# Two-layer graph attention in float32: the last step's combination of layer 0 set earlier, and its transposes placed directly behind a set of q and k

## The chip, the cores and the metric

The kernel runs on one core of a Trainium2 chip. The time is device time in microseconds (us) for one launch, given as the median of several runs. A profiled execution of the same program shows what each engine did: TensorE (PE for matmuls, PEld for its weight loads), VectorE (DVE), ScalarE (ACT), GpSimd (POOL) and SyncE (SP), which issues most of the transfers.

## The reference

There are 64 graphs of 256 nodes with 512 features, and an adjacency matrix for each. Two attention layers follow each other, both with a layer norm and a ReLU in front and a residual sum behind.

```python
# layer 0: 4 heads of 64
h = jnp.maximum(_layernorm(x), 0.0)
q, k, v = split_heads(h @ Wq), split_heads(h @ Wk), split_heads(h @ Wv)
sim = jnp.where(adj[:, None], jnp.einsum('bhid,bhjd->bhij', q, k) * 64 ** -0.5, -finfo.max)
x = x + (softmax(sim) @ v, heads joined) @ Wo + bo

# layer 1: 8 heads of 64, a second layer norm with gamma and beta inside, the diagonal always allowed
h = jnp.maximum(_layernorm(x), 0.0)
h = _layernorm(h) * gamma + beta
q, k, v = split(h @ w_qkv.T)
scores = jnp.where((adj | eye)[:, None], jnp.einsum('bihd,bjhd->bhij', q, k) * 64 ** -0.5, -1e9)
x = x + (softmax(scores) @ v, heads joined) @ w_out.T + b_out
```

(The excerpt is shortened; all of it is float32.)

## The kernel before

The 64 graphs are taken two at a time, in 32 steps (s = 0 to 31). A step has 512 tokens, which are four row blocks of 128. Two heads of 64 make a pair; layer 0 has pairs 0 and 1, layer 1 has pairs 0 to 3. The work of a step consists of the following pieces.

- `load_x` (L485) fetches the residual rows `xt`, and `first_bias` (L490) adds the bias of layer 0 to them on POOL, in four additions (L493).
- `project_qk` (L743) makes q and k of two pairs at once. It splits the product into 2x2 blocks and uses seven block products where the plain way needs eight. I call the seven products a **set**. Each product is four matmuls in float32, which the profile records as eight (L755). The products come in the order 1, 6, 5, 2, 7, 3, 4 (`SET`). Each is evicted from PSUM before it can be used: products 1 and 2 by ACT (L689, L697), products 6, 5, 7, 3 and 4 by DVE (L691, L693, L695, L699, L701). `bank_of` (L729) lets product 2 add into product 1's PSUM bank, product 3 into product 5's, and product 4 into product 7's, so product 4 can begin only when product 7 has been evicted, by L695.
- `project_v1` (L788) and `combine1` (L813) are sets too: v of layer 1 (L796), and the output projection of layer 1 (L821). `combine0` (L803) is the output projection of layer 0, in the plain way: two matmuls for each row block (L807), and the sum with `xt` on DVE (L811).
- `visit` (L986) handles one pair's attention between two sets. It weighs the values of the pair whose probabilities are ready (`weigh_out`, matmuls L896, copy on ACT L914), sums its keys (`key_sums`, L930, from the half sums `pd` that `key_halves` makes at L887), inverts the sums on DVE (`invert`, L940 and L941), sends the inverses to all rows by eight transfers on SP (L955, into the tile `invb`, which has one buffer), and multiplies them in on POOL (`normalise`, L960). For the next pair it makes the scores (L853), masks them on DVE (`mask_scores`, L877) and exponentiates on ACT (`exponentials`, L882).
- `norm1` (L615) and `norm1_rest` (L630) are the two nested layer norms before layer 1. For each row block: statistics of `xt` on DVE (L569, L570), the negated mean on ACT (L623), centring and ReLU into `h` on ACT (L624), statistics of `h` on DVE. Then for two row blocks at a time five small operations on POOL (L639, L640, and L579 to L581 in `row_scales`), and `scale_row` (L583) on ACT (L585).
- `transpose_h` (L644) turns `h` by 16 transposes on PE (L651), four for each block of 128 features; ACT (L661) and DVE (L657) evict them into `hT`. `act_sums0` and `act_sums1` (L407 to L413) make the four sums of blocks that a set needs.

The order of instructions on PE, DVE, ACT and POOL is written out by hand. Every piece is put into a list by `at(period, place, ...)`, `at_set` spreads the seven products of a set over one unit of place, and at the end the list is sorted by `period * 6.13 + place`. In one period of 6.13 units, step s does layer 1 while step s+1 finishes layer 0 and step s+2 begins it, so that a set of one step covers the DVE, ACT and POOL work of another. Each engine then runs its own list in order; semaphores make it wait for what it needs. SP has its transfers in order as well. The last period (p = 30) is special: step 30 finishes, step 31 must do the whole of its layer 1, and there is no step 32 whose work could cover it.

In that period the order on PE is: q and k of step 30's pairs 0 and 2 (place 0), v of step 30 (1), q and k of its pairs 1 and 3 (2), then `combine0` of step 31 (3), a visit (3.685), the transposes of step 31 (3.8), q and k of step 31's pairs 0 and 2 (`LAST_QK` = 4), `combine1` of step 30 (5), q and k of step 31's pairs 1 and 3 (6), v of step 31 (7), all four weighings (8) and `combine1` of step 31 (8.1). A visit stands ahead of each set up to place 3, and others between the products of later sets.

```python
            at_dense(p, AT_C0 + 0.01 + 0.14 * t - back, 0.14, combine0, s, t)
            at(p, AT_C0 + 0.3 + 0.14 * t - back if (s, t) != (NSTEP - 1, 3) else 3.69, norm1, s, t)
```

Of the kernel before, what the change touches and what calls it, by code (L numbers as in the profile page):

```python
# [315 lines left out]
def fast_path(  # L316
# [19 lines left out]
    nc = tc.nc  # L336
# [70 lines left out]
    def act_sums0(b, eng=nc.gpsimd):  # L407
        eng.tensor_tensor(b[:, 3], b[:, 7], b[:, 0], ALU.subtract)
# [334 lines left out]
    def project_qk(s, lyr, a, n):  # L743

        st = S[s]
        half, w = (PR0, PR1)[lyr] // 2, (wqk0, wqkv1)[lyr]
        if n == 1:
            for pr in (a, a + half):
                st["qk", lyr, pr] = sm.tile([P, 2, T], FP, name="qk", bufs=3)
        t0, t1 = st["qk", lyr, a], st["qk", lyr, a + half]  # L750
        bank, first = bank_of(st, ("qk", a), n, N)
        wa, ba = PRODUCT[n]
        for k in range(2):
            for c in range(HC):
                nc.tensor.matmul(  # L755
                    bank[:, k, :], w[:, wa, c, k, a * P:(a + 1) * P], st["hT"][:, ba, c, :],
                    start=first and (k, c) == (0, 0), stop=(k, c) == (1, HC - 1),
                    skip_group_check=True,
                )

        def rest():
            evacuate(n, bank, (t0[:, :, :N], t0[:, :, N:], t1[:, :, :N], t1[:, :, N:]))
            if lyr == 0 and n in (3, 4):
                t = t0 if n == 3 else t1
                nc.gpsimd.tensor_tensor(t[:, 0, :], t[:, 0, :], st["ne"], ALU.mult)
        return rest
# [203 lines left out]
    def at(period, place, fn, *args):  # L970
        events.append((period * PERIOD + place, len(events), fn, args))

    def at_dense(period, place, length, fn, *args):

        rest = []
        at(period, place, lambda: rest.append(fn(*args)))
        at(period, place + length - LAST, lambda: rest[0]())

    def at_set(period, place, order, fn, *args):
        for i, n in enumerate(order):  # L980
            at_dense(period, place + i / 7, 1 / 7, fn, *args, n)
# [1 line left out]
    SET = (1, 6, 5, 2, 7, 3, 4)  # L983
    SETC = (1, 5, 2, 6, 7, 3, 4)

    def visit(period, w, prev, cur, later=0.0):  # L986

        w -= 0.0003
        if 0 <= prev[0] < NSTEP:
            at(period, w, weigh_out, *prev)  # L990
            at(period, w, key_sums, *prev[:3])
            at(period, w + later, invert, *prev[:3])
            at(period, w + (0.63 if prev[1:3] == (1, 1) else 0.55), normalise, *prev[:3])
        if 0 <= cur[0] < NSTEP:
            at(period, w, scores, *cur)
            at(period, w + later, mask_scores, *cur, 0)
            at(period, w + 0.05, exponentials, *cur, 0)
            at(period, w + 1 / 7, mask_scores, *cur, 1)
            at(period, w + 0.18, exponentials, *cur, 1)
            at(period, w + 0.2, key_halves, *cur, 0)  # L1000
            at(period, w + 0.3, key_halves, *cur, 1)

    AT_C0, AT_Q0, AT_V0, AT_H1, AT_C1 = 3.0, 3.57, 4.57, 5.13, 5.131
    LAST_QK = 4.0
    for s in range(-1, NSTEP - 1):
        p, tail = s, s == NSTEP - 2
        if s >= 0:
            visit(p, 0.0, (s + 1, 0, 0, True), (s + 1, 0, 1))
            visit(p, 1.0, (s + 1, 0, 1, False), (s, 1, 0))
        visit(p, 2.0, (s, 1, 0, True), (s, 1, 2))  # L1010
        visit(p, 3.0, (s, 1, 2, False), (s, 1, 1))
        visit(p, 3.685 if tail else AT_Q0 + 2 / 7, (s, 1, 1, False), (s, 1, 3), 0.03 if tail else 0.0)
        if s >= 0:
            visit(p, LAST_QK + 3 / 7 if tail else AT_V0, (s, 1, 3, False), (s + 2, 0, 0))

    none = (NSTEP,)
    p = NSTEP - 2
    for w, i, pr in (
        (LAST_QK + 1, 5 / 7, 0), (LAST_QK + 1 + 3 / 7, 5 / 7, 2), (LAST_QK + 3, 5 / 7, 1), (LAST_QK + 3 + 2 / 7, 4 / 7, 3)
    ):  # L1020
        visit(p, w, none, (NSTEP - 1, 1, pr))
        at(p, w + i - 0.0005, key_sums, NSTEP - 1, 1, pr)
        at(p, w + i, invert, NSTEP - 1, 1, pr)
    for i, pr in enumerate((0, 1, 2, 3)):
        at(p, LAST_QK + 4 + 0.01 * i, weigh_last, pr)

# [5 lines left out]
    for s in range(NSTEP):  # L1032
# [33 lines left out]
        p = s - 1  # L1066
        if s == 0:
            p -= 2.23 / PERIOD
        at(p, 1.0 if s else 0.0, load_x, s)
        at(p, 1.8 if s else 1.55, first_bias, s)  # L1070
        back = 0.0 if s else 0.13
        for t in range(NT):
            at_dense(p, AT_C0 + 0.01 + 0.14 * t - back, 0.14, combine0, s, t)
            at(p, AT_C0 + 0.3 + 0.14 * t - back if (s, t) != (NSTEP - 1, 3) else 3.69, norm1, s, t)
            at(p, ((3.55, 3.7, 4.05, 4.2) if s < NSTEP - 1 else (3.55, 3.6, 3.7, 3.705))[t] - back, norm1_rest, s, t)
            at(p, 3.62 + 0.08 * t if 0 < s < NSTEP - 1 else 6.5 + 0.1 * t, second_bias, s, t)
            at(p, 4.5 + 0.1 * t if 0 < s < NSTEP - 1 else (4.25 if s == 0 else 3.71) + 0.003 * t, scale_row, s, t)

        for c in range(NC):
            at(p, (AT_H1 if s < NSTEP - 1 else 3.8) + 0.0001 * c, transpose_h, s, 1, c)  # L1080
        at(p, AT_C1 + 0.15 if s < NSTEP - 1 else 3.95, lambda s=s: act_sums0(S[s]["hT"], nc.gpsimd if s < NSTEP - 1 else nc.vector))
        at(p, AT_C1 + 0.5 if s < NSTEP - 1 else 3.96, lambda s=s: act_sums1(S[s]["hT"], nc.gpsimd if s < NSTEP - 1 else nc.vector))
        p = s
        if s < NSTEP - 1:
            at_set(p, 0.0, SET, project_qk, s, 1, 0)
            at_set(p, 1.0, SET, project_v1, s)
            at_set(p, 2.0, SET, project_qk, s, 1, 1)
            last = s == NSTEP - 2
            at(p, 4.55 if not last else LAST_QK + 0.99, lambda s=s: act_sums0(S[s]["oT1"]))
            at(p, AT_C1 + 0.1 if not last else LAST_QK + 1.0, lambda s=s: act_sums1(S[s]["oT1"]))  # L1090
            at_set(p, AT_C1 if not last else LAST_QK + 1, SETC, combine1, s)
            at(p, 6.3, store, s)
        else:
            p = s - 1
            at_set(p, LAST_QK, SET, project_qk, s, 1, 0)
            at_set(p, LAST_QK + 2, SET, project_qk, s, 1, 1)
            at_set(p, LAST_QK + 3, SET, project_v1, s)
            at(p, LAST_QK + 4.015, lambda s=s: act_sums0(S[s]["oT1"], nc.vector))
            at(p, LAST_QK + 4.035, lambda s=s: act_sums1(S[s]["oT1"], nc.vector))
            at_set(p, LAST_QK + 4.1, (1, 5, 2, 3, 6, 7, 4), combine1, s)  # L1100
            for n, (i, j) in enumerate(((0, 0), (0, 1), (1, 1), (1, 0))):
                at(p, LAST_QK + 4.1 + (3, 6, 6, 7)[n] / 7, store_block, s, i, j)
# [69 lines left out]
```

## Time and profile before

| | |
|---|---|
| median of 3 runs | 3401.17 us (3400.61 to 3402.93) |
| the profiled execution: its time, its span | 3401.54 us, 3399.3 us |
| PE busy | 3373.3 us, 99% of the span |
| PEld, DVE, ACT, POOL busy | 77%, 56%, 37%, 59% |
| transfers | 173.89 MB, 51 GB/s in the mean |
| the chain of work that ended last | PE 97%, DVE 1% |

The page gives busy time by engine over the whole span. The chain of work that ended last is followed back from the last instruction, at each step to what released it. The timeline lists instructions of one engine in order of time: start, length, line and operation, and in brackets the idle time before it with what ended that. Matmuls overlap, and their ends are modelled. The windows table gives busy time and the granted PE clock (1.00 is full speed) in stretches of time.

### The profile page before, as it was taken

How to read it: one execution, taken by the hardware profiler on the slowest of the kernel's cores; microseconds unless marked ns; L12 is line 12 of the kernel's file. 1: busy time of each engine (PE TensorE's matmuls, PEld its weight loads, DVE VectorE, ACT ScalarE, POOL GpSimd, SP SyncE). 2: the span in 40 equal slices, each digit the busy share in tenths (PEclk: the TensorE clock that was granted, in tenths of full speed). 3: DMA queues.
4: the chain of work that ended last, by engine and by line, in shares of the span. 5: the costliest groups of instructions: out<-in, count | busy, mean ns of one | idle time of the engine just before them, and what ended most of it. 6: DMA issues, size and time to landing. Idle time of an engine off the chain costs nothing.

```text
span 3399.3 us, 59198 instructions
## 1 busy us (share of the span) xinstructions
PE 3373.3 (99%) x22602; PEld 2621.7 (77%) x22602; DVE 1919.5 (56%) x3402; ACT 1243.2 (37%) x2193; POOL 1991.2 (59%) x1858
## 2 busy tenths in 40 slices
PE   8999999999999999999999999999999999999999
PEld 6777777787777877778777777777787777877777
DVE  6755556555565555555555655556555555555565
ACT  4433443333333334433344333343333443334431
POOL 5655665556655556655576556665555655556632
PEclk9999999999999999999999999999999999999999
DMA  4111111211111211111111111111121111111111
GB/s 129 46 56 57 48 39 46 58 57 54 32 48 56 58 54 33 48 55 56 58 43 44 46 58 57 53 32 48 57 58 52 34 47 57 57 58 41 32 41 42
DMA packets 167697, 173.89 MB, mean 51 GB/s; under 512 B 59624, under 2 KB 112368, under 8 KB 167408
## 3 DMA queue, kind: packets, MB, share of 16 engines
q1 hardware_dynamic: 167008, 169.78, 16.9%
q8 instruction: 180, 2.95, 0.4%
q14 instruction: 109, 0.89, 0.1%
q10 hardware_dynamic: 400, 0.27, 0.0%
HBM read 85.99 MB, written 33.62 MB: 35 GB/s over the span
## 4 chain that ended last, share of the span: by engine, by line
PE 97%; DVE 1%; ACT 0%; issue 0%; DMA 0%; POOL 0%; SPq 0%; DVEq 0%; POOLq 0%
PE mm L755 34%; PE mm L796 12%; PE mm L821 11%; PE sc L853 11%; PE sc L896 10%; PE mm L782 6%; PE mm L807 6%; PE mm L651 3%; PE mm L930 2%; PE mm L543 0%; DVE bs L569 0%; ACT h L585 0%; DVE wqk L405 0%; DVE wqkv L405 0%; DVE inv L940 0%
## 5 line engine op out<-in xcount | busy, mean ns | idle before, releaser
L887 POOL TENSOR_TENSOR pd<-p 128x512 f32<-128x512 f32 x378 | 477.2, 1278 | 631.6 <-ACT p L882 523.3
L755 PE MATMUL mm<-hT,wqkv 128*128 128x256 f32 x3584 | 800.0, 382 | 2.6 <-DVE hT L411 1.4
L755 PEld LDWEIGHTS mm<-hT,wqkv 128*128 128x128 f32 x3584 | 673.8, 190 | 112.6 <-issue 23.1
L882 ACT ACTIVATE p<-p 128x512 f32<-128x512 f32 x768 | 459.1, 629 | 478.8 <-DVE p L877 477.9
L940 DVE RECIPROCAL inv<-mm 128x128 f32<-128x128 f32 x384 | 339.7, 926 | 367.6 <-PE mm L930 330.9
L877 DVE TENSOR_TENSOR p<-sc,n 128x512 f32<-128x512 f32 x768 | 481.2, 682 | 4.2 <-PE sc L853 4.2
L914 ACT COPY oT<-sc 128x512 f32<-128x512 f32 x188 | 110.2, 586 | 993.6 <-PE sc L896 993.6
L755 PE MATMUL mm<-hT,wqk 128*128 128x256 f32 x1792 | 403.4, 382 | 0.7 <-ACT wqkv L468 0.6
L796 PE MATMUL mm<-wqkv,hT 128*128 128x256 f32 x1792 | 396.1, 381 | 0.0
L821 PE MATMUL mm<-wo,oT 128*128 128x256 f32 x1792 | 393.3, 379 | 1.0 <-DVE xt L712 0.7
L960 POOL TENSOR_TENSOR oT<-oT,invb 128x512 f32<-128x512 f32 x188 | 240.9, 1282 | 261.0 <-DMA invb<-inv 253.3
L755 PEld LDWEIGHTS mm<-hT,wqk 128*128 128x128 f32 x1792 | 338.4, 191 | 69.5 <-DVE inv L940 9.9
L853 PE MATMUL sc<-qk 64*128 64x256 f32 x3072 | 384.1, 389 | 0.0
L796 PEld LDWEIGHTS mm<-wqkv,hT 128*128 128x128 f32 x1792 | 337.6, 190 | 56.3 <-issue 11.4
L821 PEld LDWEIGHTS mm<-wo,oT 128*128 128x128 f32 x1792 | 337.6, 190 | 47.7 <-issue 1.5
L896 PE MATMUL sc<-p,v 128*32 128x256 f32 x6144 | 370.7, 382 | 0.0
L853 PEld LDWEIGHTS sc<-qk 64*128 64x128 f32 x3072 | 281.2, 186 | 104.2 <-issue 77.6
L896 PEld LDWEIGHTS sc<-p,v 128*32 128x32 f32 x6144 | 180.3, 109 | 162.0 <-issue 61.5
L723 POOL TENSOR_TENSOR xt<-xt,u 128x512 f32<-128x512 f32 x93 | 118.1, 1270 | 245.6 <-DVE xt L716 183.9
L585 ACT ACTIVATE h<-h,mr,r 128x512 f32<-128x512 f32 x252 | 197.4, 809 | 115.4 <-POOL mr L581 115.3
L782 PE MATMUL mm<-wv,hT 128*128 128x256 f32 x1024 | 230.3, 382 | 0.0
L807 PE MATMUL mm<-wo,oT 128*128 128x512 f32 x512 | 230.3, 593 | 0.0
(123 smaller groups left out, 3675.1 us busy)
## 6 DMA issues: line engine op xcount, KB each, us to landing
invb<-inv SPq DMA_DIRECT2D x1528, 32.0 KB, 1.8
xt<-in_x_dram SPq DMA_DIRECT2D x32, 1024.0 KB, 9.8
h<-in_x_dram SPq DMA_DIRECT2D x31, 1024.0 KB, 6.2
out_dram<-xt SPq DMA_DIRECT2D x31, 1024.0 KB, 4.5
ne<-row SPq DMA_DIRECT2D x30, 256.0 KB, 4.4
ad<-in_adj_dram SPq DMA_DIRECT2D x32, 128.0 KB
wr<-in_L_gnn_w_qkv_dram SPq DMA_DIRECT2D x3, 1024.0 KB, 13.5
h<-in_x_dram SPq DMA_DIRECT2D x4, 256.0 KB, 2.7
```

Source lines behind the costliest of these rows:

```text
L755: nc.tensor.matmul(bank[:, k, :], w[:, wa, c, k, a * P:(a + 1) * P], st["hT"][:, ba, c, :], start=first and (k, c) == (0, 0), stop=(k, c) ...
L782: nc.tensor.matmul(bank, st["hT"][:, b0 + t // NIC * step, c % HC, i:i + P], wv0[:, c, :], start=(c == 0), stop=(c == NC - 1),)
L796: nc.tensor.matmul(bank[:, t, :], st["hT"][:, ba, c, t * P:(t + 1) * P], wqkv1[:, wa, c, 2, :], start=first and (t, c) == (0, 0), stop=(t, ...
L807: nc.tensor.matmul(bank, st["oT0"][:, pr, t // NIC, t % NIC * P:(t % NIC + 1) * P], wo0[:, pr, :], start=(pr == 0), stop=(pr == PR0 - 1),)
L821: nc.tensor.matmul(bank[:, t, :], st["oT1"][:, ba, c, t * P:(t + 1) * P], wo1[:, wa, c, :], start=first and (t, c) == (0, 0), stop=(t, c) ...
L853: nc.tensor.matmul(sc[g][e][:, kc, :], qk[rows, 1, k0:k0 + P], qk[rows, 0, g * N:(g + 1) * N], start=True, stop=True,)
L877: nc.vector.tensor_tensor(p[e][:, g], sc[e], neg[:, :, g, :], ALU.add)
L882: nc.scalar.activation(p[e][:, g], p[e][:, g], AF.Exp, scale=SCALE)
L887: eng.tensor_tensor(pd[:, e], p[e][:, :, 0, :], p[e][:, :, 1, :], ALU.add)
L896: nc.tensor.matmul(po[r0:r0 + 32, g, :], st[f"v{lyr}"][:, g * NIC + kc, pr * P + r0:pr * P + r0 + 32], p[r0 // DH][:, g, kc, :], start=(kc ...
L940: nc.vector.reciprocal(inv[:, i * P:(i + 1) * P], sums[:, i * P:(i + 1) * P])
L960: nc.gpsimd.tensor_tensor(dst, dst, invb, ALU.mult)
```

## The change

All that moves is in the last period, and concerns step 31 and the end of step 30.

- `combine0` of step 31 goes from place 3 to just ahead of the visit at place 2, so a set earlier. `load_x` moves from 1.0 to 0.7 and `first_bias` from 1.8 to 1.25.
- `norm1`, `norm1_rest` and `scale_row` of step 31 go into the set at place 2 (q and k of step 30's pairs 1 and 3), and the transposes and the sums of `hT` come directly behind that set, ahead of the visit at place 3.
- `LAST_QK` becomes 3: q and k of step 31's pairs 0 and 2 follow at 3, of its pairs 1 and 3 at 4, `combine1` of step 30 at 5, v of step 31 at 6, the weighings at 7. The two sets of q and k now follow each other, and `combine1` of step 30 comes behind both. The visits of the tail are placed anew, and the visit at 3 + 4/7 loses its delay.
- One more pair's q and k are alive at a time than the three `qk` buffers hold. Pairs 0 and 2 of step 31 are therefore written into `wqk0`, the weights of layer 0, which are not needed any more.

```diff
         if n == 1:
-            for pr in (a, a + half):
-                st["qk", lyr, pr] = sm.tile([P, 2, T], FP, name="qk", bufs=3)
+            for i, pr in enumerate((a, a + half)):
+                if (s, lyr, a) == (NSTEP - 1, 1, 0):
+                    tile_qk = wqk0[:, 2 * i:2 * i + 2].rearrange("p n c k o -> p n (c k o)")
+                else:
+                    tile_qk = sm.tile([P, 2, T], FP, name="qk", bufs=3)
+                st["qk", lyr, pr] = tile_qk
...
-    LAST_QK = 4.0
+    LAST_QK = 3.0
...
-        visit(p, 3.685 if tail else AT_Q0 + 2 / 7, (s, 1, 1, False), (s, 1, 3), 0.03 if tail else 0.0)
+        visit(p, LAST_QK + 4 / 7 if tail else AT_Q0 + 2 / 7, (s, 1, 1, False), (s, 1, 3))
         if s >= 0:
-            visit(p, LAST_QK + 3 / 7 if tail else AT_V0, (s, 1, 3, False), (s + 2, 0, 0))
+            visit(p, LAST_QK + 1 if tail else AT_V0, (s, 1, 3, False), (s + 1, 1, 0) if tail else (s + 2, 0, 0))
...
-    for w, i, pr in (
-        (LAST_QK + 1, 5 / 7, 0), (LAST_QK + 1 + 3 / 7, 5 / 7, 2), (LAST_QK + 3, 5 / 7, 1), (LAST_QK + 3 + 2 / 7, 4 / 7, 3)
-    ):
-        visit(p, w, none, (NSTEP - 1, 1, pr))
-        at(p, w + i - 0.0005, key_sums, NSTEP - 1, 1, pr)
-        at(p, w + i, invert, NSTEP - 1, 1, pr)
+    for w, i, pr in ((1, 5 / 7, 0), (1 + 3 / 7, 5 / 7, 2), (2, 5 / 7, 1), (2 + 3 / 7, 5 / 7, 3)):
+        if pr:
+            visit(p, LAST_QK + w, none, (NSTEP - 1, 1, pr))
+        at(p, LAST_QK + w + i - 0.0005, key_sums, NSTEP - 1, 1, pr)
+        at(p, LAST_QK + w + i, invert, NSTEP - 1, 1, pr)
...
-        at(p, 1.0 if s else 0.0, load_x, s)
-        at(p, 1.8 if s else 1.55, first_bias, s)
+        at(p, 0.0 if s == 0 else 1.0 if s < NSTEP - 1 else 0.7, load_x, s)
+        at(p, 1.55 if s == 0 else 1.8 if s < NSTEP - 1 else 1.25, first_bias, s)
         back = 0.0 if s else 0.13
         for t in range(NT):
-            at_dense(p, AT_C0 + 0.01 + 0.14 * t - back, 0.14, combine0, s, t)
-            at(p, AT_C0 + 0.3 + 0.14 * t - back if (s, t) != (NSTEP - 1, 3) else 3.69, norm1, s, t)
-            at(p, ((3.55, 3.7, 4.05, 4.2) if s < NSTEP - 1 else (3.55, 3.6, 3.7, 3.705))[t] - back, norm1_rest, s, t)
+            if s == NSTEP - 1:
+                at_dense(p, 1.9991 + 0.00013 * t, 0.0011, combine0, s, t)
+            else:
+                at_dense(p, AT_C0 + 0.01 + 0.14 * t - back, 0.14, combine0, s, t)
+            at(p, AT_C0 + 0.3 + 0.14 * t - back if s < NSTEP - 1 else (2.2, 2.25, 2.4, 2.45)[t], norm1, s, t)
+            at(p, ((3.55, 3.7, 4.05, 4.2) if s < NSTEP - 1 else (2.3, 2.35, 2.5, 2.55))[t] - back, norm1_rest, s, t)
...
-            at(p, 4.5 + 0.1 * t if 0 < s < NSTEP - 1 else (4.25 if s == 0 else 3.71) + 0.003 * t, scale_row, s, t)
+            at(p, 4.5 + 0.1 * t if 0 < s < NSTEP - 1 else 4.25 + 0.003 * t if s == 0 else 2.6 + 0.01 * t, scale_row, s, t)
 
         for c in range(NC):
-            at(p, (AT_H1 if s < NSTEP - 1 else 3.8) + 0.0001 * c, transpose_h, s, 1, c)
-        at(p, AT_C1 + 0.15 if s < NSTEP - 1 else 3.95, lambda s=s: act_sums0(S[s]["hT"], nc.gpsimd if s < NSTEP - 1 else nc.vector))
+            at(p, (AT_H1 if s < NSTEP - 1 else 2.9995) + 0.00001 * c, transpose_h, s, 1, c)
+        at(p, AT_C1 + 0.15 if s < NSTEP - 1 else 2.9996, lambda s=s: act_sums0(S[s]["hT"], nc.gpsimd if s < NSTEP - 1 else nc.vector))
...
-            at_set(p, AT_C1 if not last else LAST_QK + 1, SETC, combine1, s)
+            at_set(p, AT_C1 if not last else LAST_QK + 2, SETC, combine1, s)
...
             at_set(p, LAST_QK, SET, project_qk, s, 1, 0)
-            at_set(p, LAST_QK + 2, SET, project_qk, s, 1, 1)
+            at_set(p, LAST_QK + 1, SET, project_qk, s, 1, 1)
             at_set(p, LAST_QK + 3, SET, project_v1, s)
```

## The prediction

> **What bounds the kernel now.** The page comes first: PE is busy for 3373.3 of 3399.3 us, so all that a reordering can win back is idle or slow PE time.
>
> ```profile
> span 3399.3 us, 59198 instructions
> ...
> PE 3373.3 (99%) x22602; PEld 2621.7 (77%) x22602; DVE 1919.5 (56%) x3402; ACT 1243.2 (37%) x2193; POOL 1991.2 (59%) x1858
> ```
>
> Where is that time? The list of waits of PE, cut to the last 250 us, has four lines, and all belong to the stage that the change touches.
>
> ```profile
> PE mm L651 <- ACT h L585: 3.0, 4, 1.7
> PE mm L755 <- DVE hT L411: 1.4, 1, 1.4
> PE mm L821 <- DVE xt L712: 0.7, 1, 0.7
> PE mm L821 <- POOL oT L408: 0.3, 1, 0.3
> ```
>
> The timeline of PE shows the place, and the windows table the granted clock there (it is the number ahead of the last two).
>
> ```profile
> 3297.17 2.52 PE L853 MATMUL sc<-qk 64*128 64x256 f32 x16
> 3300.41 0.33 PE L651 MATMUL mm<-ident,h 128*128 128x128 f32 x1 [0.73 <-ACT h L585]
> 3301.12 0.33 PE L651 MATMUL mm<-ident,h 128*128 128x128 f32 x1 [0.38 <-ACT h L585]
> 3303.14 0.48 PE L651 MATMUL mm<-ident,h 128*128 128x128 f32 x1 [1.69 <-ACT h L585]
> 3303.84 3.03 PE L651 MATMUL mm<-ident,h 128*128 128x128 f32 x13 [0.23 <-ACT h L585]
> 3306.68 3.25 PE L755 MATMUL mm<-hT,wqkv 128*128 128x256 f32 x8
> 3311.34 3.69 PE L755 MATMUL mm<-hT,wqkv 128*128 128x256 f32 x16 [1.42 <-DVE hT L411]
> ```
>
> ```profile
> 3301.00:3302.00 1.00, 0.33 (x1) 0.14 (x1) 1.00 (x2) 0.07 (x1) 0.89 (x2) 1.00 0.00 0
> 3302.00:3303.00 1.00, 0.00 (x0) 0.00 (x0) 0.96 (x4) 0.73 (x2) 0.20 (x1) 0.79 0.00 0
> 3303.00:3304.00 1.00, 0.63 (x2) 0.34 (x3) 1.00 (x4) 1.00 (x3) 0.00 (x0) 0.50 0.13 32
> ...
> 3308.00:3309.00 1.00, 1.00 (x4) 0.81 (x3) 1.00 (x3) 0.64 (x2) 0.00 (x0) 0.50 0.13 33
> 3309.00:3310.00 1.00, 0.92 (x4) 0.42 (x2) 0.90 (x2) 0.63 (x2) 0.93 (x1) 0.79 0.00 0
> ```
>
> The reader is to see two losses: the transposes wait for the layer norm row by row, and the idling halves the clock for some 6.8 us. Until 3314.96, when the next weighing begins, 17.79 us pass. Undisturbed, this work takes 8.95: scores 1.93, 16 transposes 1.75, three products of 12.28 / 7 = 1.755 each (all from the undisturbed chain of work). That is a loss of 8.8, or 8.7 if 0.14 is allowed for the switch to the weighing (16 records of L755 ahead of one take 3.65 instead of 3.51). A second loss is the first product of `combine1`, 2.32 us from 3326.29 to 3328.61 instead of 1.73: 0.6, most of it the wait on L408. **Together 9.3 us can be had here.** The 0.7 on L712 is in step 31's own `combine1`, whose order stays.
>
> **What the skill says.** The Trainium skill, "TensorE: Matmul & The Clock Gate", Part 1: The HAM clock gate, says that an idle window of about 3.4 us brings the clock to half, and that the window runs freely. The trace agrees: half clock holds from 3302.58 to 3309.42, two such windows, and the window ahead (3299.17 to 3302.58) had PE busy for 1.2 us, 35%. The one from 3309.42 to 3312.83 had 58% and cost nothing. The same page (Architectural detail) calls ACT and DVE strict first-in-first-out: an eviction that stands behind layer-norm work waits for it. "SBUF — State Buffer" (its single rule) says that a DVE instruction with two SBUF inputs and a reading GpSimd instruction exclude each other. Here L411 takes 1.57 us beside POOL's L887, and 0.69 at 3380.68 where POOL rests.
>
> **The change part by part.** The number of instructions of each engine and of transfers is the same, so PE's work is the same and only waits count. I set V as the start of the weighing of step 30's pair 0: 3267.15 before, and 7.06 later (L807 from 3287.81 to 3294.87) after, as `combine0` now precedes it.
>
> *Combination earlier.* The load of `xt` doesn't move on SP's queue: it waits for the store of step 29 in either case, is issued at 3248.1, and the transfers are quiet again by 3252.7. The four bias additions (4.95 us) now stand on POOL between the two half sums: 3258.24 + 1.25, + 4.95, + 1.25, and the normalisation of layer 0's pair 1 (1.27) ends at 3266.9, where before it ended at 3262.6. `combine0` starts at 3267.1 and needs that pair 0.9 later. Cost 0, cover 0.9 us; without it, delays go straight to PE. The four sums on DVE (0.69) end before the reciprocals at V + 2.4.
>
> *Layer norm inside the set.* Queued on DVE behind the masks (end V + 7.06, as 3274.14 is to 3267.08) are eight statistics of 0.80 (L569 to the next instruction), with the evictions of products 6 and 5 (0.6 from start to start) among them. Starts: rows 0 and 1 at 7.0 and 7.8; L691 8.6; their `h` (ACT begins at 8.0, needs 0.2 + 0.7 each) 9.2 and 10.0; row 2 10.8; L693 11.6; row 3 12.2; `h` of row 2 13.1; `h` of row 3 14.2, as ACT ends it at 14.1; then L695, 15.0 to 15.7. L693 is done at 12.3, ahead of product 3 at 13.0. **But product 4 should start at V + 4.22 + 6 x 1.755 = 14.75 and must wait for L695: a new wait of 1.0 us, PE on DVE L695.** Behind it queue the transposes, and on DVE L699, L701 and L657.
>
> *Transposes.* After the last statistics (aggregate at 14.9) POOL needs 1.85 (3300.39 to L585's start at 3302.27), so ACT scales rows 2 and 3 from 16.8 to 18.3. PE comes to them at 17.5 with rows 0 to 2 ready and waits for row 3 until 18.35; 13 more of 0.11 end at 19.8. Unstalled it is 4.22 + 12.28 + 1.75 = 18.25. **New loss 1.55 us**, nearly independent of the wait on L695, as the row chain sets the end.
>
> *The sums of `hT`* end on DVE at 23.3 (POOL idle, so 0.69 each), behind a visit of 4.22 that holds PE until 24.0: the 1.42 wait is gone. The reciprocals of pair 2 come 1.1 late, which nobody on PE feels.
>
> *The tail.* Visits now stand three products apart (9.5 us), and each round of inverses takes 8.3 us from reciprocal to normalisation (3269.51 to 3277.80), in one buffer. I worked them through with X as the fourth visit (V + 40.5). Pair 3's half sums are ready 0.5 before its key sums. Its transfers wait until X + 10.3 for POOL's normalisation of pair 1 behind a half sum, so the reciprocals of step 31's pair 0 start at X + 16.75 instead of 15.6, and L699 ends at X + 19.6, where the second half of the next scores needs it at X + 20.1. Product 4 of `combine1` waits for L712 with 0.45 to spare. POOL's L408 is 1.7 early, so that the 0.6 is won too. SP's store of step 30 now stands ahead of the last inverses, which land more than 8 us before their use. Cost 0; bounds 0 and, if every slack fails by half a us, 1.5.
>
> *q and k in `wqk0`.* A view instead of a tile; its last reader ran a period earlier. Nothing.
>
> **Sum:** 9.3 - 1.55 = 7.75 us less. Profiled: span 3399.3 to 3391.5, its time 3401.54 to 3393.8. The median of the runs is 0.37 below the profiled time, so 3401.17 - 7.75 = **3393.4 us**.
>
> **Rivals.**
> 1. *Clock drops again.* The two new waits (1.0 and 0.55) lie within 3.56 us, so a window has at worst 1.4 idle, 59% busy: just above the 58% seen harmless. If it drops, two windows at half clock cost 6.8 x 0.5 = 3.4: gain 4.35, 3396.8. For it: the phase is free. Against: 35% is the only case seen that dropped.
> 2. *A tail slack fails.* The slacks of 0.45 to 0.5 us above are near the error of my offsets. It costs 0.3 to 1.5: 3393.7 to 3394.9.
> 3. *No new wait at all*, if ACT and POOL run ahead of my offsets: 9.3 gained, 3391.9. Against: L695 really stands behind eight statistics.
> 4. *Slower: the single `invb` buffer becomes the bound.* If each round takes e longer than the 6.4 us from first issue to landing that I used, the reciprocals of step 31's pair 2 come 2e later, and PE feels 2e less about 0.45 at product 4 of `combine1`. That eats the whole gain from e = 4.1 us; at e = 8 it costs 15.5, and the time is 3409. Against it: these transfers land 1.7 to 1.9 us after issue at every place in the tail.
> 5. *It does not move PE's wait:* the bias on POOL or the load is late, and `combine0` stalls as long as the norm did. It needs more than 0.9 us at once, and 8 to undo all. The load is seven us early.
>
> **How the numbers follow.** Forecast (3392.6 to 3394.2): 0.55. Rival 1: 0.14. Rival 2: 0.17. Rival 3: 0.08. Rival 4: 0.03. Rival 5: 0.03, near 3400. 0.2% is 6.8 us, about what a measurement of this kernel can tell from no change; it lies only 0.95 inside the forecast. Faster than that: 0.52 of the forecast's share, all of rival 3 and half of rival 2, 0.68. Slower by as much, beyond 3408: part of rival 4, 0.02. Within it: 0.30. The range for 8 in 10 leaves out rivals 4 and 5 and the outer edges: 3391.7 to 3397.0, which takes in both ends of the unknown costs.
>
> **What would show it.** PE's waits after should hold one on DVE L695 near 1.0 and one or two on ACT L585 of about 0.5 together; those on L411 and L408 should be gone, and L712's 0.7 stay. The sixteen transposes should end 19.8 us after the weighing of pair 0 begins, and the clock should read 1.00 throughout. `combine0` should start within 0.1 of the end of v's set. The weighing of all four pairs, 3372.78 before, should start near 3365.0. The forecast is wrong if the clock falls to 0.5 in the set, if PE waits for L960 (POOL's normalisation) at `combine0`, or if a wait on L699, L712 or POOL's half sums of over 0.5 us shows in the tail.

## The result and the profile after

The changed kernel takes 3393.55 us in the median (3392.93 to 3395.45), beside 3402.34 (3400.61 to 3403.35) for the kernel before on the same chip. The ratio is 0.9975, with a 95% interval of 0.9966 to 0.9985: about 8.8 us faster. The ten times of the kernel before fall into two groups of five (3400.61 to 3401.79 and 3402.88 to 3403.35), those of the changed kernel into eight and two (3392.93 to 3393.87, and 3394.66 and 3395.45), so a part of the 8.8 is this mixture: the medians of the lower groups, 3401.11 and 3393.35, are 7.8 apart. The profiled execution took 3393.86 us, with a span 7.3 us shorter than before.

In the changed kernel's file the lines named here from L755 on stand 4 lower, so that L755 of before is L759 here, L807 is L811, L821 is L825, L853 is L857, L887 is L891, L896 is L900, L914 is L918, L940 is L944, L955 is L959 and L960 is L964. L651, L585 and L691 to L723 keep their numbers.

The page of the kernel after, its first lines:

```profile
span 3392.0 us, 59193 instructions
...
PE 3369.1 (99%) x22602; PEld 2619.0 (77%) x22602; DVE 1915.7 (56%) x3402; ACT 1243.1 (37%) x2193; POOL 1988.2 (59%) x1858
```

PE's work is the same 22602 records, busy for 4.2 us less. In the kernel before, PE was busy for 6.04 of the 6.83 us at half clock; at full clock that work would take half as long, so an estimated 3.0 of the 4.2 is the clock. The waits of PE in the last 250 us, in total, times and longest:

```profile
PE mm L759 <- DVE qk L695: 0.8, 1, 0.8
PE mm L825 <- DVE xt L712: 0.7, 1, 0.7
PE sc L857 <- DVE qk L699: 0.3, 1, 0.3
PE mm L651 <- ACT h L585: 0.3, 1, 0.3
```

The waits of 3.0 on the layer norm (L585), 1.4 on L411 and 0.3 on L408 have become 0.3, nothing and nothing. Two waits are new, on L695 and L699. The timeline of PE shows where (start, duration, and in brackets the idle time before):

```profile
3267.24 7.03 PE L811 MATMUL mm<-wo,oT 128*128 128x512 f32 x16
...
3289.83 1.99 PE L759 MATMUL mm<-hT,wqkv 128*128 128x256 f32 x8 [0.78 <-DVE qk L695]
...
3292.47 1.64 PE L651 MATMUL mm<-ident,h 128*128 128x128 f32 x13 [0.31 <-ACT h L585]
3294.04 1.93 PE L900 MATMUL sc<-p,v 128*32 128x256 f32 x32
...
3335.84 1.14 PE L857 MATMUL sc<-qk 64*128 64x256 f32 x8 [0.34 <-DVE qk L699]
...
3365.70 7.11 PE L900 MATMUL sc<-p,v 128*32 128x256 f32 x128
```

`combine0` starts at 3267.24, as soon as the set of v is done. Sixteen transposes end at 3294.04, behind one short wait. DVE shows why product 4 waited: L695 was in the queue behind the statistics.

```profile
3288.29 0.69 DVE L569 BATCH_NORM_STATS2 bs<-h 128x6 f32<-128x512 f32 x1 [0.23 <-ACT h L624]
3289.12 0.66 DVE L695 TENSOR_TENSOR qk<-mm,qk 128x512 f32<-128x512 f32 x1
```

L411, 1.57 us before, takes 0.69 at 3295.66, since no half sum runs on POOL beside it. The windows table has a clock of 1.00 in every us from 3286 to 3306, even from 3289 to 3290, where PE was busy for 0.22 us.

**The stage.** From here on I compare one length read from each trace. It runs from the end of the set of v of step 30 (where `combine0`, or in the old order the weighing of step 30's pair 0, begins) to the start of the weighing of all four pairs. Before it is 3372.78 - 3267.08 = 105.70 us, after it is 3365.70 - 3267.24 = 98.46: 7.24 less. The 0.7 on L712 lies behind the stage, in every list of waits alike.

In the fourteen profiled executions of this document the stage begins between 3266.70 and 3269.62. Five of them (evict_first, normalise_first, both_later, early_sums and filled_sums_first) have a stretch of 3.4 us at half clock near the start of the kernel, between 20.9 and 25.9 us, and their stages begin at 3268.91 or later; the nine others have none and begin at 3267.68 or earlier. The times of one kernel spread over 2 to 4 us. So effects below one us are read from the length of the stage and not from medians. Each length comes from a single execution, and I trust it where the waits in the trace account for it.

### The profile page after: what moved, and what is told of

Its sections match the earlier page's. It is cut to its first block, busy times and chain, and to the rows that moved or that the text cites. A ratio compares the mean times of both kernels' runs of the same rounds, so it can differ in the third digit from the quotient of the medians.

```text
span 3392.0 us, 59193 instructions
## 1 busy us (share of the span) xinstructions
PE 3369.1 (99%) x22602; PEld 2619.0 (77%) x22602; DVE 1915.7 (56%) x3402; ACT 1243.1 (37%) x2193; POOL 1988.2 (59%) x1858
## 4 chain that ended last, share of the span: by engine, by line
PE 97%; DVE 2%; ACT 0%; issue 0%; DMA 0%; SPq 0%; POOL 0%; DVEq 0%; POOLq 0%
PE mm L759 34%; PE mm L800 12%; PE mm L825 11%; PE sc L857 11%; PE sc L900 10%; PE mm L786 6%; PE mm L811 6%; PE mm L651 3%; PE mm L934 2%; PE mm L543 0%; DVE bs L569 0%; DVE inv L944 0%; ACT h L585 0%; DVE wqk L405 0%; DVE p L881 0%
## 5 line engine op out<-in xcount | busy, mean ns | idle before, releaser
L891 POOL TENSOR_TENSOR pd<-p 128x512 f32<-128x512 f32 x378 | 476.2, 1274 | 646.0 <-ACT p L886 537.7
L759 PE MATMUL mm<-hT,wqkv 128*128 128x256 f32 x3584 | 799.1, 381 | 2.0 <-ACT wo L468 1.2
L759 PEld LDWEIGHTS mm<-hT,wqkv 128*128 128x128 f32 x3584 | 672.6, 190 | 112.4 <-issue 21.5
L944 DVE RECIPROCAL inv<-mm 128x128 f32<-128x128 f32 x384 | 339.8, 926 | 368.6 <-PE mm L934 339.1
L918 ACT COPY oT<-sc 128x512 f32<-128x512 f32 x188 | 110.2, 586 | 994.0 <-PE sc L900 980.7
L759 PE MATMUL mm<-hT,wqk 128*128 128x256 f32 x1792 | 403.3, 382 | 0.8 <-ACT wqkv L468 0.6
L825 PE MATMUL mm<-wo,oT 128*128 128x256 f32 x1792 | 393.3, 379 | 0.7 <-DVE xt L712 0.7
L759 PEld LDWEIGHTS mm<-hT,wqk 128*128 128x128 f32 x1792 | 338.4, 191 | 69.6 <-DVE inv L944 9.9
L964 POOL TENSOR_TENSOR oT<-oT,invb 128x512 f32<-128x512 f32 x188 | 240.1, 1277 | 243.0 <-DMA invb<-inv 235.7
L857 PE MATMUL sc<-qk 64*128 64x256 f32 x3040 | 379.8, 389 | 0.3 <-DVE qk L699 0.3
L825 PEld LDWEIGHTS mm<-wo,oT 128*128 128x128 f32 x1792 | 337.6, 190 | 47.4 <-issue 1.5
L900 PE MATMUL sc<-p,v 128*32 128x256 f32 x6144 | 370.7, 382 | 0.0
L857 PEld LDWEIGHTS sc<-qk 64*128 64x128 f32 x3040 | 277.9, 186 | 103.7 <-issue 77.3
L900 PEld LDWEIGHTS sc<-p,v 128*32 128x32 f32 x6144 | 180.3, 109 | 161.8 <-issue 62.1
L723 POOL TENSOR_TENSOR xt<-xt,u 128x512 f32<-128x512 f32 x93 | 118.1, 1270 | 256.3 <-DVE xt L716 183.9
L585 ACT ACTIVATE h<-h,mr,r 128x512 f32<-128x512 f32 x252 | 197.4, 809 | 114.8 <-POOL mr L581 114.7
L811 PE MATMUL mm<-wo,oT 128*128 128x512 f32 x512 | 230.2, 592 | 0.0
```

Source lines behind the costliest of these rows:

```text
L759: nc.tensor.matmul(bank[:, k, :], w[:, wa, c, k, a * P:(a + 1) * P], st["hT"][:, ba, c, :], start=first and (k, c) == (0, 0), stop=(k, c) ...
L811: nc.tensor.matmul(bank, st["oT0"][:, pr, t // NIC, t % NIC * P:(t % NIC + 1) * P], wo0[:, pr, :], start=(pr == 0), stop=(pr == PR0 - 1),)
L825: nc.tensor.matmul(bank[:, t, :], st["oT1"][:, ba, c, t * P:(t + 1) * P], wo1[:, wa, c, :], start=first and (t, c) == (0, 0), stop=(t, c) ...
L857: nc.tensor.matmul(sc[g][e][:, kc, :], qk[rows, 1, k0:k0 + P], qk[rows, 0, g * N:(g + 1) * N], start=True, stop=True,)
L891: eng.tensor_tensor(pd[:, e], p[e][:, :, 0, :], p[e][:, :, 1, :], ALU.add)
L900: nc.tensor.matmul(po[r0:r0 + 32, g, :], st[f"v{lyr}"][:, g * NIC + kc, pr * P + r0:pr * P + r0 + 32], p[r0 // DH][:, g, kc, :], start=(kc ...
```

## Experiments

My theory is that the gain is the layer norm's stall, its half clock and the wait on the sums (L411), all moved behind other work, less a row chain that ends 1.55 us late. Three questions follow: are the leftovers what I say they are, does either half of the change do it alone, and can the leftovers be removed?

### What is left: the row chain

**rows_early.** The statistics of the norm directly behind `combine0`'s rows, ahead of the visit (edit shortened):

```diff
-  norm1      at (2.2, 2.25, 2.4, 2.45)[t]
-  norm1_rest at (2.3, 2.35, 2.5, 2.55)[t]
+  norm1      at 1.99921 + 0.00013 * t
+  norm1_rest at (1.99935, 1.99948, 1.99961, 2.1)[t]
```

> The statistics of step 31's rows, and the centring on ACT, stand directly behind each sum of the combination, where DVE idles for 1.0 us at a time, instead of inside the set of q and k. My theory (the chain statistics, h, statistics, POOL, scaling sets the end of the transposes and the eviction of product 7 stands behind it): both new waits of PE, 0.78 on L695 and 0.31 on L585, vanish; the transposes end 18.3 us after the weighing of pair 0 begins instead of 19.84; the last weighings start 1.5 us earlier than 3365.7; time about 1.5 us below the changed kernel. Rival (PE only catches its breath there, other waits take their place, such as the reciprocals or the copy of the weighing on ACT behind the row work): less than 0.7 us gained, with a new wait at the scores of pair 2.

Measured: 3394.33 us (3393.33 to 3395.81), ratio to before 0.9979 (0.9972 to 0.9986), a stage of 98.22. The waits on L695 and L585 are gone, the 0.3 on L699 stays, and only 0.24 is won. This is what the rival said, and not my theory: the transposes end 19.65 us after the weighing of pair 0 begins, where I expected 18.3. A wait of PE and the timeline of ACT show what took their place:

```profile
PE sc L857 <- ACT oT L918: 0.7, 1, 0.7
```

```profile
3277.72 0.20 ACT L623 ACTIVATE mv<-mv 128x1 f32<-128x1 f32 x1 [1.37 <-DVE mv L570]
...
3278.58 0.56 ACT L918 COPY oT<-sc 128x512 f32<-128x512 f32 x1
```

ACT's queue held row 3's centring ahead of the copy of the weighing (L918). ACT stood 1.37 us for row 3's statistics, and the scores behind L918 took 3.32 us instead of 1.93. One early row too many gave the gain back on another engine; both_later, below, takes that row alone out.

**evict_first.** The other way round: the evictions L695 and those before it ahead of row 3's second statistics (`norm1_rest` of row 3 from 2.55 to 2.72, `scale_row` of rows 2 and 3 to 2.73 and 2.74).

> The eviction of product 7 (L695) stands ahead of the last row's second statistics instead of behind them. Theory (the row chain sets the end, the wait on L695 only takes a share of it): PE's wait on L695 goes from 0.78 to 0, the wait on L585 grows by as much and by a further 0.3 to 0.4, since the last statistics start that much later; transposes end 20.2 us after the weighing of pair 0 begins instead of 19.84; time the same or 0.4 us above the changed kernel. Rival (the eviction is the cause): 0.8 us below the changed kernel.

Measured: 3394.32 us (3393.11 to 3396.16), ratio 0.9978 (0.9969 to 0.9987), a stage of 98.70, 0.24 more than after. L695 has no wait and L585 has 1.4 (1.01 and 0.38). The transposes end 20.08 us after the weighing of pair 0 began, beside 19.84 after. So the wait on L695 costs nothing of its own: the last row's chain sets the end of the transposes, as the prediction said.

**two_more_stats.** Two more statistics of row 3 on DVE, ahead of L695, whose results nobody reads:

```diff
+        for _ in range(2 if (s, t) == (NSTEP - 1, 3) else 0):
+            bs = stat.tile([P, 6], FP, name="bs")
+            nc.vector.bn_stats(bs, h[:, t, :])
```

> Two statistics of the last row are made twice more than needed, with no use of the result: the row chain is 1.4 us longer. Theory: the wait on L695 becomes 2.2 us and the transposes end 1.4 us later; PE is then idle for 2.5 us of about 5, and a window of 3.4 us can have as little as 35% to 45% of busy time, so the clock may fall to half; time 1.4 us above the changed kernel if it holds, about 4.8 us above if it falls. If the chain does not set the end, less than 0.7 us above.

Measured: 3396.23 us (3395.19 to 3397.44), ratio 0.9983 (0.9976 to 0.999), a stage of 101.02, 2.56 more than after. The wait on L695 (L698 here) grew from 0.78 to 1.97, and the clock fell for one window, which put the result between my two expectations of 1.4 and 4.8. The windows table shows it:

```profile
3292.00:3293.00 1.00, 1.00 (x5) 0.85 (x4) 0.00 (x0) 0.78 (x2) 0.19 (x1) 0.66 0.00 0
3293.00:3294.00 1.00, 1.00 (x4) 0.71 (x4) 0.13 (x1) 0.74 (x2) 0.00 (x0) 0.50 0.00 0
```

(The columns are PE, PEld, DVE, ACT and POOL busy, then the granted clock.) 1.4 us of DVE work in that place cost 2.56 on PE. Product 4 starts 1.19 later; from there to the end of the transposes, mostly at half clock, PE takes 1.13 more, although the wait on the scaling is gone; and the wait in the tail is 0.58 instead of 0.34 (L702 here, L699 in the kernel after). The fall of the clock is rival 1 of the prediction: one longer wait on DVE was enough to bring it about.

### What is left: the tail

**normalise_first.** In the tail the late normalisation on POOL (0.63 of a set behind its visit) goes back to 0.55, ahead of both half sums (edit shortened):

```diff
-  normalise at w + (0.63 if prev[1:3] == (1, 1) else 0.55)
+  normalise at w + (0.63 if prev[1:3] == (1, 1) and prev[0] < NSTEP - 2 else 0.55)
```

> POOL normalises step 30's pair 1 ahead of the half sums of step 31's pair 0, not between them. Theory (single buffer of inverses: the eight transfers of pair 3 wait for this normalisation, the next reciprocals for the transfers, L699 for the reciprocals): the 0.34 wait of PE's second half of the scores on L699 vanishes, the reciprocals of step 31's pair 0 start about 1 us or more earlier, time 0.3 to 0.5 us below the changed kernel. Rival (L699 is late because DVE has too much in that stretch): the wait stays.

Measured: 3393.18 us (3392.7 to 3395.03), ratio 0.9976 (0.9967 to 0.9986), a stage of 97.85, 0.61 less than after. The wait on L699 is gone and the others are as they were. The chain of work that ended last, in the kernel after, shows what it was (start, length, what):

```profile
3323.97 1.28 POOL oT L964
...
3328.36 0.59 SPq L959
...
3328.99 1.76 SPq L959
...
3330.79 1.88 DMA invb<-inv
```

POOL's normalisation L964 frees the only `invb` behind a half sum. SP then issues eight transfers, and the seventh issue takes 1.76 us instead of 0.6; the eighth starts behind it, at 3330.79, and lands 1.88 later. The reciprocals of the next pair wait for the landing, and L699 stands on DVE behind them. The four traces with this order (after, rows_early, evict_first, two_more_stats) all have one issue of 1.7 to 2.0 us in this round and a wait on L699 of 0.29 to 0.58; the three with the earlier normalisation (normalise_first, both, both_later) have no issue above 0.6 and no such wait. So the edit took both delays away. Why one issue takes three times as long in that place is not known.

**both.** rows_early and normalise_first together.

> Row statistics behind each sum of the combination, and the normalisation of step 30's pair 1 ahead of the half sums of step 31's pair 0, in one kernel. Theory: both parts add, no wait of PE is left in the last period but the 0.7 on L712: 1.9 us below the changed kernel, 9.1 below the kernel before by the traces. Rival (they share a cause): no more than the better of the two alone.

Measured: 3394.31 us (3393.06 to 3395.65), ratio 0.9977 (0.9969 to 0.9985), a stage of 97.65, 0.81 less than after. That is about the sum of the two alone (0.24 and 0.61), so they do add; the 1.9 that I expected did not come because the list of waits keeps L918 (0.7), beside L712 (0.7).

**both_later.** The same, with row 3 alone taken out of the early rows (edit shortened):

```diff
-  norm1      at 1.99921 + 0.00013 * t
-  norm1_rest at (1.99935, 1.99948, 1.99961, 2.1)[t]
+  norm1      at (1.99921, 1.99934, 1.99947, 2.16)[t]
+  norm1_rest at (1.99935, 1.99948, 1.99961, 2.3)[t]
```

> The kernel after with the late normalisation of pair 0 put ahead of the half sum, as before, and the layer norm of rows 0 to 2 taken directly behind combine0's rows; row 3's statistics come after the first visit's masks and its scaling on ACT after the exponentials. Theory (L918's new wait came only from row 3's ACT work standing ahead of it): L918 copies out at once, the scores take 1.9 us, and L695, L585 and L699 have no wait, so that L712's 0.7 alone is left in the list. The stage from combine0's start to the four weighings would be 96.6 to 97.0 us, 1.5 to 1.9 below the kernel after, and the median about 3392. Rival (the wait of 0.7 on L918 moves on to the next of these, L695 or L585, because row 3's two statistics again stand behind masks): a stage of 97.5 or more.

Measured: 3392.24 us (3391.14 to 3394.17) beside 3401.53 for the kernel before, ratio 0.9973 (0.9962 to 0.9983). The stage is 96.26, 2.20 less than after. The list of waits of PE for the last 250 us has one line left, and the timeline has no gap between `combine0` and the four weighings:

```profile
PE mm L825 <- DVE xt L712: 0.7, 1, 0.7
```

```profile
3269.41 7.03 PE L811 MATMUL mm<-wo,oT 128*128 128x512 f32 x16
...
3294.62 1.93 PE L900 MATMUL sc<-p,v 128*32 128x256 f32 x32
...
3365.67 7.11 PE L900 MATMUL sc<-p,v 128*32 128x256 f32 x128
```

So the leftovers of the change are known: the transposes end 18.26 us after the first weighing here and 19.84 after (1.58), and the scores that waited for L699 end 0.62 later after, counted from the fourth visit (21.94 against 21.32). Together 2.20, the whole difference. By the trace this is the best version; by the medians it can't be told from the kernel after (9.29 and 8.79 below the kernel before of their own comparisons, with intervals some 3.5 us to each side).

### Which half of the change does it

**early_only.** The kernel before with only the combination, the norm, the bias and the load earlier (the transposes at 3.5, the visit at 3.685 without its delay, the sums of `hT` left at 3.95 and the sets as they were).

> From the kernel before: only the combination, the layer norm and the bias go a set earlier; the sets behind keep their order (q and k of step 31's pairs 0 and 2, the output projection of step 30, then the other q and k), and the transposes stand between the two visits, which have no set between them any more. Theory: the norm's stall and the half clock go, 8.7 us; the wait on L695 (0.8) comes; the visits without a set between them cost about 2.5 us (weighing waits for exponentials 1.1, key sums for the half sums 1.35); L408's 0.6 stays lost. Net 5.4 below the kernel before, 1.9 above the changed kernel. Rival (the earlier combination alone is the whole gain): 7 below the kernel before.

Measured: 3402.66 us (3401.42 to 3405.2), ratio 1.0002 (0.9994 to 1.0011), a stage of 105.89: nothing gained, where I expected 5.4. The stall on L585 is gone, and PE waits 3.68 us for L411 instead, which my expectation had not seen. The timelines of PE and DVE show the wait and what stands ahead of the sums:

```profile
3309.65 5.41 PE L755 MATMUL mm<-hT,wqkv 128*128 128x256 f32 x16 [3.68 <-DVE hT L411]
```

```profile
3302.58 1.77 DVE L940 RECIPROCAL inv<-mm 128x128 f32<-128x128 f32 x2 [2.38 <-PE mm L930]
...
3304.84 2.48 DVE L877 TENSOR_TENSOR p<-sc,n 128x512 f32<-128x512 f32 x4
3307.24 0.68 DVE L408 TENSOR_TENSOR hT<-hT 128x512 f32<-128x512 f32 x1
3308.02 1.57 DVE L411 TENSOR_TENSOR hT<-hT 128x512 f32<-128x512 f32 x1
```

DVE had evicted its share of the transposes by 3300.2, but did the reciprocals and masks of the next visit first. L408 starts 40.05 us into the stage, only 1.7 sooner than before (41.76). PE came to that point much earlier, idled for 3.68 us, and the clock fell behind it: the two products after the wait take 5.41 us instead of 3.69. The 1.7 is given back there, and the next weighing starts 47.8 us into the stage, as before (47.9).

**early_sums.** The same with the sums directly behind the transposes (`act_sums0` and `act_sums1` from 3.95 and 3.96 to 3.501 and 3.502).

> The early combination and layer norm alone, with the sums of hT on DVE taken directly behind the transposes, ahead of the masks of the next visit; the sets stay in their old order. Theory (in the run without this, only the sums' place on DVE stood in the way): the wait of 3.7 on L411 is gone, the clock stays at 1.00, waits of about 0.8 on L695 and 0.3 to 0.6 on L408 are left, and the stage is 101 to 102.5 us, about 3.5 below before. Rival (the sums then hold up the visit's reciprocals and masks by as much as they gain): 104.5 us or more.

Measured: 3398.94 us (3396.99 to 3400.27), ratio 0.9991 (0.9984 to 0.9998), a stage of 102.77. The gain of 2.93 is a little less than expected. The wait on L411 is gone and the clock stays at 1.00, but the waits of PE have new lines:

```profile
PE mm L821 <- POOL oT L408: 1.8, 1, 1.8
PE mm L930 <- POOL pd L887: 1.1, 1, 1.1
```

In the old order of the sets, two visits stand on the two sides of the transposes with no set between them (scores at 3296.33, the next weighing at 3300.15), so the half sums of the first (L887, 3.04 us for two beside DVE's sums) are needed before POOL has made them. And `combine1` of step 30 follows one set later, where the changed order has two, so that its sums on POOL (L408) come 1.8 late. By the timeline, the weighing and the key sums behind the transposes take 4.74 us here (3300.15 to 3304.89) and 2.29 in the kernel after (3294.04 to 3296.33), and from the first product of `combine1` to the next instruction 3.84 pass and not 1.92. Together that is 4.4 us, about the 4.31 by which the stage is longer than after.

**sets_only.** The other half: the order of the last sets as in the change, all of `combine0`, norm and transposes as before.

> From the changed kernel: the combination, layer norm and transposes are put back to where they were before; kept are the two sets of q and k of step 31 behind each other, the output projection of step 30 behind both, and q and k in the tile of the old weights. Theory: the norm's stall and the half clock are back, only L408's 0.6 us is won: 0.6 below the kernel before, not to be told from it. Rival (the order of the sets gives a good part): 2 us or more below.

Measured: 3406.67 us (3405.71 to 3408.36), ratio 1.0015 (1.0008 to 1.0021). This run does not answer its question: I had left the store of step 30 at place 6.3, ahead of the end of its projection. Some of that step's last sums are missing from what is stored, and DVE's L714 stood behind the store, which put two new waits (3.2 on L934, 2.0 on L825) into the list.

**sets_only_2.** The same with that store at 7.3, so that it holds all of the sums.

> The kernel before with only the order of the last sets changed: the q and k of both halves back to back, the combination of step 30 behind them, and that step's store behind its last product. Combination and layer norm of step 31 stay where they were. Theory (the gain is the layer norm's stall of 8.7 us, the order of the sets is worth only the 0.6 on L408): waits on L585 of about 3 and on L411 of about 1.4 stay, the clock falls to half around 3302 to 3310, and the stage from the weighing of step 30's pair 0 to the four weighings is 105.0 to 106.0 us. Rival (the sets' order is where the gain comes from): 100 us or less.

Measured: 3400.6 us (3399.46 to 3402.78), ratio 0.9998 (0.9989 to 1.0007), a stage of 104.70, 1.0 less than before. Waits of PE:

```profile
PE mm L651 <- ACT h L585: 3.0, 4, 1.7
PE mm L759 <- DVE hT L411: 2.7, 1, 2.7
```

The norm's stall stays, and the 0.6 at L408 is won; 0.2 of the rest is won ahead of the product that waits for L411, which starts 44.05 us into the stage and not 44.26. The clock happened to fall for one window only (3302.84 to 3306.26), and yet L411's wait grew to 2.7: PE was faster and waited longer for the same sums on DVE.

Neither half does all of it alone: 2.93 (with the sums moved) and 1.0, but 7.24 together. The early norm needs the new order of the sets, which puts a whole set between the visits and a second set of q and k ahead of `combine1`.

### Is it the idling of PE, or DVE's queue?

**before_filled.** The kernel before with eight matmuls that nobody reads in the gap ahead of the transposes, so that the clock does not fall there.

> The kernel before with eight matmuls of 128x256 more on PE, ahead of the transposes of step 31, whose result nobody reads: 3.5 us of added work where PE idled for 3.0. Theory (the idling halved the clock, and this cost 3.4 of the 9.3 us): the clock stays 1.00, the 13 last transposes take 1.5 instead of 3.03 us and the first product after them 1.8 instead of 3.25; the wait on L411 takes back a part, as DVE's chain is not faster; time 2 to 3 us below the kernel before although work is added. Rival (the clock only went along with waits that would be there anyway): the same time as before, or up to 0.5 above.

Measured: 3401.77 us (3399.14 to 3403.22), ratio 1.0 (0.9991 to 1.0008), a stage of 105.98. That is the rival's figure, but not for the rival's reason: the transposes ran at full clock, as I expected. Then:

```profile
3305.22 1.99 PE L755 MATMUL mm<-hT,wqkv 128*128 128x256 f32 x8
3309.55 5.38 PE L755 MATMUL mm<-hT,wqkv 128*128 128x256 f32 x16 [2.34 <-DVE hT L411]
```

The first product ends 40.5 us into the stage, 2.35 sooner than before. Of that 0.9 went into a longer wait on L411 (2.34 instead of 1.42), and the rest into the clock, which fell after all, one gap later (3310.38 to 3313.80): 5.38 us for two products instead of 3.69. DVE's sums, behind the masks and beside POOL's half sums, leave a gap of their own that is long enough to bring the clock down.

**filled_sums_first.** The same with the sums of `hT` moved to 3.8275, meant to be ahead of the visit's second masks.

> The kernel before with eight more matmuls, which nobody reads, in the gap ahead of the transposes, and besides with the sums of hT ahead of the next visit's second masks on DVE. Theory (with the clock held up, only the sums behind the masks kept the filled kernel from gaining): the wait on L411 falls from 2.3 to 0.6 or less, the clock stays at 1.00 to the end of the stage, and the stage is 101.5 to 103 us, about 3 to 4 below before. Rival (masks that come later hold up the scores of the visit, or the sums are slow beside POOL's L887 whatever their place): 104.5 us or more.

Measured: 3399.66 us (3398.16 to 3401.31), ratio 0.9994 (0.9986 to 1.0003), a stage of 103.24: 2.46 gained, and a clock of 1.00 throughout. The wait left on L411 is 1.27, more than expected. DVE shows that the edit had put only the first of the sums ahead of the masks:

```profile
3308.78 0.68 DVE L408 TENSOR_TENSOR hT<-hT 128x512 f32<-128x512 f32 x1
3309.38 1.28 DVE L877 TENSOR_TENSOR p<-sc,n 128x512 f32<-128x512 f32 x2
3310.58 0.68 DVE L411 TENSOR_TENSOR hT<-hT 128x512 f32<-128x512 f32 x1
```

The 1.27 that remains is about the 1.28 of those masks. What helped is not an early start of L411: it begins 40.96 us into the stage, beside 41.14 in before_filled. But it takes 0.68 instead of 1.57, because the masks, and with them POOL's half sum (L887 at 3310.81), now come later and L411 begins 0.23 ahead of that half sum. So the wait is 1.07 shorter, and the clock, which no longer falls, gives the other 1.69 back. Filling alone gains nothing; it pays once the next gap is short enough. The moved sum without the filling was not tried. It could win at most the wait of 1.42 on L411 in the kernel before, so at least 1.0 of the 2.46 needs both.

## Why the prediction was right, point by point

- **The time.** Forecast 3393.4, measured 3393.55. That it is so close is partly luck: the base was 3401.17 in the three runs shown and 3402.34 beside the changed kernel, while the medians differ by 8.79 and the stage gave 7.24 where I had 7.75. The profiled executions differ by 7.68.
- **9.3 us can be had.** Confirmed by both_later, which has none of these losses and no new ones: 105.70 - 96.26 = 9.44. What my sum did not show is that its terms don't come singly: with PE's stall alone taken away (before_filled, early_only) nothing is won, since PE then waits 2.34 or 3.68 us for DVE's sums and the clock halves behind that gap. The change moves the sums with the transposes, and so the total held.
- **Combination earlier, at no cost.** Held: `combine0` starts where the set of v ends, and POOL's last normalisation of layer 0 ends at 3267.13, 0.2 later than I had it and still ahead of that start.
- **A new wait of 1.0 on L695.** It is 0.78: L695 ended at 15.58 and not 15.7 us after the weighing began, and PE came to product 4 at 14.85 and not 14.75.
- **Transposes end at 19.8.** They end at 19.84. The statement that the row chain and not L695 sets that end was confirmed by evict_first. The loss of 1.55 measured 1.58 against both_later. The wait on L585 is 0.31 and not 0.55: the first three transposes took 0.49 us where I had 0.33, and row 3 came 0.08 earlier.
- **The sums of `hT`.** Held: 0.69 for L411, no wait.
- **The tail at cost 0.** This is the one step that failed, within its bounds of 0 to 1.5. The slack of 0.5 at L699 was not there: I had used 6.4 us from the first issue of `invb` to its landing, and this round took 7.4 (3325.28 to 3332.67), as the seventh of its eight issues on SP took 1.76. Reciprocals that I had at 16.75 us after the fourth visit began at 17.98. The wait is 0.34, and its cost in the stage 0.62, by normalise_first 0.61. The slacks at L712 and at the half sums held.
- **The four weighings near 3365.0.** They start at 3365.70: 0.62 later from L699, 0.16 later because the set of v ended that much later in this execution, and some 0.1 earlier from small differences.
- **Rivals.** The second (a slack fails) was true in part, beside the forecast. The first (the clock) did not happen, but two more statistics on DVE were enough to bring it about. The third (no new wait) did not happen; both_later has no new wait, but by another order of the rows. The fourth (a longer round of `invb`) happened by 1.0 us, far from the 4.1 at which it would have eaten the gain. The fifth did not happen.

## What to carry to other kernels

When a stalled engine is given its input earlier, follow the work on to the next queue that it passes: here the norm's stall and DVE's sums behind the masks were two limits one behind the other, and removing the first alone gained nothing. Where work is pulled ahead in an in-order queue, take as much of it as arrives in time and no more: with three of four rows early (both_later) the stage is 1.4 us shorter than with all four (both). A slack taken as the difference of two offsets is safe only down to the spread of the transfers that it contains, here 1 us in a round of eight.

## What the runs showed of the hardware

**When the clock falls.** The Trainium skill, "TensorE: Matmul & The Clock Gate", Part 1: The HAM clock gate, speaks of a free-running window of about 3.4 us and of an idle one that halves the clock. The length agrees: the half-clock stretches of early_only, before_filled, sets_only_2 and two_more_stats each last 3.41 to 3.42 us. But none of the windows ahead of them was idle throughout, nor was the one of 35% in the kernel before that the prediction names. From the timelines, PE was busy for 0.84 of 3.42 us (25%) ahead of the one in sets_only_2, for 29% in early_only, 32% in before_filled and 42% in two_more_stats, and each time the clock fell. It stayed at 1.00 after windows that were 58% busy (kernel before) and 60% (sets_only_2, 3306.26 to 3309.68).

Between these the share does not decide alone. In sets_only the clock fell at 3302.41 and again at 3363.85, which is 18 windows of 3.413 us apart, as a free-running window would have it. If such windows are counted from the fall in each trace, the clock also fell after 45% (sets_only, 3299.00 to 3302.41), 48% (both_later, 18.86 to 22.27) and 50% (early_sums, 19.09 to 22.50), but it stayed at 1.00 after 46% (sets_only, 3353.61 to 3357.02) and 53% (sets_only, 3309.24 to 3312.65). Nor does the length of one gap decide: in sets_only PE idled for 3.25 us without a break ahead of L934, and the clock stayed, since the gap was shared by two windows of 46% and 58%. What else counts, such as the busy time of weight loads, was not tried.

The way back asks for more. In the kernel before, the first window at half clock was 77% busy and a second one at half clock followed; the same happened after 66% in sets_only. In sets_only_2 the half-clock window was 88% busy, and the clock was full behind it.

**POOL and DVE.** "SBUF — State Buffer" of the Trainium skill, under "Who interferes with whom", says that GpSimd reading SBUF and a DVE instruction with two SBUF inputs exclude each other. L411 took 1.57 us next to a half sum on POOL in early_only, early_sums, sets_only_2 and before_filled and 0.69 in the kernel after, with POOL idle. In filled_sums_first it took 0.68, having begun 0.23 us ahead of the half sum. The half sums pay too: two took 3.04 us in early_sums beside DVE's sums and 2.50 in normalise_first without them.
